# A selective-scan kernel: the loads of delta * x issued from ScalarE's queue, right behind an exponential, with six tiles in place of five

## The chip, the cores and the metric

The kernel runs as one program on one core of a Trainium2 chip. The metric is the time of one execution on the device in microseconds (us); three executions of the kernel before gave 13694.4, 13700.04 and 13704.54 us, a median of 13700.04 us. The engines are called as in the profile: PE (TensorE, matrix products), DVE (VectorE), ACT (ScalarE), POOL (GpSimd) and SP (SyncE, which here only issues DMAs). Each has an instruction stream of its own, worked off in order[...].

## The reference, cut to what matters

Four layers are computed one after the other on a batch of four 64 x 64 images with 128 channels. Layers 0 and 1 hold a selective scan in four directions; layers 2 and 3 (a gated neighbourhood message and a neighbourhood attention) are not touched by the change. The scan, for every image, direction k, channel d and state n (16 states):

```python
def step(h, t):
    x_t, d_t, B_t, C_t = t
    h = jnp.exp(d_t[..., None] * A) * h + (d_t * x_t)[..., None] * B_t[:, :, None, :]
    return (h, jnp.einsum('bkdn,bkn->bkd', h, C_t))
```

Here d_t is delta = softplus(...), x_t the convolved input, and the sequence has 64 * 64 = 4096 positions in each direction. Layer 0 has 128 channels, layer 1 has 256.

## The kernel before, in words

**Tiling.** A task is one image and one block of 128 channels of one layer: 4 images x (1 + 2) blocks make 12 tasks. A task has 16 steps (4 directions x 4 pieces of 1024 positions), a step has 16 units. A unit is 8 channels x 16 states = 128 partitions by 1024 positions. So there are 12 x 16 x 16 = 3072 units, worked in order u = 0, 1, 2, ... by `Scans.run` (line 567).

**One unit.** Five things happen to a unit, each on another engine:

- `load(u)` (line 429, the DMA on line 436) brings delta * x of the unit's 8 channels from DRAM, each row repeated for the 16 states: a tile `dub` of 128 x 1024 f32, 512 KB. The rows lie in the DRAM tensor `dud`, which was stored for the whole step (line 401).
- `times_b(u)` (line 443, POOL) multiplies `dub` by B (`repB`) into one half of a pair tile `h` (three pairs in rotation).
- `decay(u)` (lines 451 and 453) spreads delta over the partitions with two products on PE into the PSUM tile `da` (two in rotation), and ACT takes the exponential in place.
- `scan(u)` (line 462, DVE) runs the recurrence along the 1024 positions over `da` and the half of `h`; after every second unit DVE multiplies the pair by C (line 472).
- `add_up`, `keep` and `save` sum over states on PE, copy sums and end states on ACT.

**Order of emission.** Nothing reorders instructions: each engine's stream is the order in which the Python code emits. Iteration u of `run` emits `scan(u)`, `times_b(u+3)`, `save`, `decay(u+2)`, `add_up`, `keep`, then pieces of the preparation of a later step (`prepare`, 22 units ahead) and pieces of "side" work (the layers' projections, convolutions and norms), and at its very end `load(u+6)`. A small planner (`Plan`, `Lane`) decides from estimated times which pieces are emitted when, and when a store that was posted is emitted. `load(u)` of the first unit of a step first emits any preparation store still posted (`plan.flush("prep")`).

**DMAs.** Before, every DMA of the program is issued by SP, so SP's stream mixes the 3072 `dub` loads with stores and loads of the preparation (`dud`, `dp<-parts` twelve for each step, `xdd`, `repB`) and of the side work (`pad`, `szd`, `xcd`, ...). SP waits in order: a DMA that waits keeps all later ones back. There are two kinds of wait. A `dub` load waits until its tile is free: with five tiles, `load(u+6)` waits for `times_b(u+1)`. And the framework hands eight completion semaphores to the DMAs in turn, in the order of emission, whichever engine issues; a DMA waits until the one that held its semaphore before, that is the eighth DMA before it, has landed. The records of the trace show this turn: the semaphores of successive DMAs are 101 to 108, then 101 again.

The two functions and their caller, with the lines as the profile counts them:

Of the kernel before, what the change touches and what calls it, by code (L numbers as in the profile page):

```python
# [219 lines left out]
class ScanWeights:  # L220
# [27 lines left out]
    def load(self):  # L248

        nct, most = self.nct, max(TILES)  # L250
        tile = self.pool.tile([P, most * ND * (H + P)], F32, name="xpdt", tag="xpdt", bufs=1)
        self.xp = tile[:, 0 : nct * ND * H].rearrange("p (t k h) -> p t k h", t=nct, k=ND)
        at = most * ND * H
        self.dtw = tile[:, at : at + ND * nct * P].rearrange("p (k c) -> p k c", k=ND)
        self.nc.sync.dma_start(out=self.xp, in_=self.d_xp)
        for i in range(HALVES):
            self.nc.sync.dma_start(out=self.dtw[i * H : i * H + self.rank], in_=self.d_dtw)
# [19 lines left out]
class Scans:  # L277
# [151 lines left out]
    def load(self, u):  # L429
        t, step, jj, j, g = self.unit(u)  # L430
        if g == 0:
            self.plan.flush("prep")
        dud = t.prepared[step]["du"]
        dub = self.live["dub", u] = self.tile("dub", 5)
        src = bass.AP(dud.tensor, dud.offset + 8 * g * TS, [[0, NS], [TS, 8], [1, TS]])
        self.nc.sync.dma_start(out=dub, in_=src)

    def times_b(self, u):
        t, step, jj, j, g = self.unit(u)
# [127 lines left out]
    def run(self, between):  # L567

        total = NU * len(self.tasks)
        first = self.tasks[0]  # L570
        first.W.load()
        for _ in self.fetch(first):
            pass
        for _ in self.prepare(first, 0):
            pass
        self.plan.start()
        pieces, fetch, fetched = Lane(self.plan, "prep", iter(())), iter(()), 0
        for u in range(-7, total):
            if u >= 0:
                self.scan(u)  # L580
            if 0 <= u + 3 < total:
                self.times_b(u + 3)
            if u >= 0 and u % NG == 0:
                self.bring_c(u)
            if u > 0 and u % 2 == 0:
                self.save(u // 2 - 1)
            if 0 <= u + 2 < total:
                self.decay(u + 2)
            if u > 0 and u % 2 == 0:
                self.add_up(u // 2 - 1)  # L590
            if u > 0 and u % 8 == 0:
                self.keep(u - 1)
            if u > 0 and u % 8 == 1:
                self.sum_so_far(u - 1)
            even, eighth, first_one = u % 2 == 0, u % 8 == 1, u % NG == 0
            self.plan.slot(
                u, 1.6 * even + 1.0 * eighth + 2.0 * first_one, 0.25 * even + 0.7 * (u % 8 == 0)
            )
            ahead, rest = divmod(u + AHEAD, NG)
            if rest == 0:  # L600
                while pieces.step():
                    pass
                self.plan.flush("prep", "rep")
            if rest == 0 and 0 < ahead < total // NG:
                n, step = divmod(ahead, NU // NG)
                if step == 0 and self.tasks[n].W is not self.tasks[n - 1].W:
                    self.tasks[n].W.load()
                if step == 0 and fetched < n:
                    fetch, fetched = self.fetch(self.tasks[n]), n
                    for _ in range(self.tasks[n].W.nct):  # L610
                        next(fetch, None)
                pieces = Lane(self.plan, "prep", self.prepare(self.tasks[n], step))

            n, step = divmod(ahead + 1, NU // NG)
            if step == 0 and fetched < n < len(self.tasks) and self.tasks[n - 1].x_done:
                fetch, fetched = self.fetch(self.tasks[n]), n
            next(fetch, None)
            while (pieces.count < rest - 4 or pieces.fits()) and pieces.step():
                pass
            if u >= 0:  # L620
                n, i = divmod(u, NU)
                if self.later:
                    self.later.pop(0)()
                between(n, i)
            if 0 <= u + 6 < total:
                self.load(u + 6)
        self.add_up(total // 2 - 1)
        self.save(total // 2 - 1)
        self.keep(total - 1)
        while self.later:  # L630
            self.later.pop(0)()


class Side:
# [142 lines left out]
    def halves(self, load):  # L777

        tiles = []

        def start(n):
            pad = self.tile("pad", shape=(P, HW // 2 + 2, HW), bufs=2)
            load(pad, n)
            tiles.append((pad, self.nc.now + ROWS_LANDING))

        start(0)
        return tiles, start

    def depthwise(self, w, bias, src, dst):
# [12 lines left out]
        def load(pad, m):  # L802
            i, half = divmod(m, 2)
            for dy in range(3):
                self.rows(pad, slice(dy * n, (dy + 1) * n), src[i * n : (i + 1) * n], half * HW // 2 + dy - 1, HW // 2)

        tiles, start = self.halves(load)
        for m in range(8):
            i, half = divmod(m, 2)
# [817 lines left out]
def layer2(tc, C, nb, x_in, x_out, d_w, d_rel, d_v, beside):  # L1627
    with ExitStack() as es:
# [11 lines left out]

        with tc.manual_schedule():
            run(statistics(0, range(8)))
            E.roots([E.rstd])
            run(project(0, range(4)))
            beside()

# [24 lines left out]
            third, second, last = halves[-3:]  # L1671
            gates = E.gates(out, last[2], [third[2]["var"]], [])
            run(merged(gates, E.finish(*third) + E.outputs(*second)))
            run(E.gather(*last, alone=True))
            E.roots([second[2]["var"]])
# [509 lines left out]
```

## Time and profile before

| What | Value |
|---|---|
| median of three runs | 13700.04 us |
| the profiled execution's own time | 13702.12 us |
| its span, first to last instruction | 13699.8 us |
| the stretch from the first to the last scan | 204.7 to 11443.2 us (11238.5 us) |
| PE, DVE, ACT, POOL busy over the span | 73%, 86%, 58%, 72% |
| mean granted TensorE clock | 0.737 |
| DMA busy share over the span | 73.6%, 181 GB/s |

How to read it: "busy" is the time in which an engine works on an instruction; instructions that only wait, branch or issue a DMA are not counted. A group line names the source line, the engine, the operation, what it writes and reads, the count, then busy time and the mean of one in ns, then the idle time of the engine just before these instructions and what ended most of it. A line of waits reads: who waited, on which line, for whom, microseconds in total, number of times, the longest. "SPq" is SP's queue, that is, the waiting or issuing of DMAs. Layers 0 and 1 fill the time up to some 11,450 us, and layers 2 and 3 the rest.

### The profile page before, as it was taken

To read this page: it belongs to the slowest core of one execution; us is meant where nothing else is said; L and a number is where in the kernel's file an instruction comes from. 1 tells how busy PE (TensorE), PEld (TensorE's weight loads), DVE (VectorE), ACT (ScalarE), POOL (GpSimd) and SP (SyncE) were. 2 spreads that over 40 slices of the span, in tenths; PEclk is the share of its full clock that TensorE was granted. 3 is DMA by queue.
4 is the path that set the end of the run, shared out by engine and by line. 5 is a ranking of instruction groups with operands and counts; after the bars stand their busy time and mean duration, and the time that the engine had idled before them with its cause. 6 is when DMAs were issued, how large, how long until landed. Compare 5 with 4: busy or idle time off the path is not lost. (4 is left out here: it accounts for less than half of the span.)

```text
span 13699.8 us, 121257 instructions
## 1 busy us (share of the span) xinstructions
PE 10024.2 (73%) x37178; PEld 2510.6 (18%) x37178; DVE 11766.7 (86%) x6980; ACT 7913.4 (58%) x10594; POOL 9928.8 (72%) x4754
## 2 busy tenths in 40 slices
PE   5777777777777777767777677777777776666688
PEld 1111111111111111111111111111111111111455
DVE  3998899989999899989999899999999994577555
ACT  3666566655665466645665555555555554665577
POOL 3787788878887788868887888888888884355200
PEclk7666767776777776667777777777777776888899
DMA  5888888898888888888889888878888784234300
GB/s 153 204 213 217 208 207 219 214 216 201 204 219 207 193 216 202 211 212 199 196 215 220 210 197 199 203 192 202 202 197 201 193 194 107 70 97 107 73 20 17
DMA packets 877057, 2474.92 MB, mean 181 GB/s; under 512 B 142455, under 2 KB 164095, under 8 KB 868215
## 3 DMA queue, kind: packets, MB, share of 16 engines
q1 hardware_dynamic: 876407, 2467.18, 73.6%
q8 instruction: 295, 4.83, 0.2%
q14 instruction: 355, 2.91, 0.1%
HBM read 2043.34 MB, written 272.37 MB: 169 GB/s over the span
## 5 line engine op out<-in xcount | busy, mean ns | idle before, releaser
L443 POOL TENSOR_TENSOR h<-dub,repB 128x1024 f32<-128x1024 f32 x3072 | 7176.1, 2357 | 1307.6 <-DMA dub<-dud 945.6
L462 DVE TENSOR_TENSOR_SCAN h<-da,state,h 128x1024 f32<-128x1024 f32 x2304 | 5324.5, 2340 | 493.6 <-POOL h L443 225.2
L453 ACT ACTIVATE da<-da,av 128x1024 f32<-128x1024 f32 x3072 | 3339.6, 1088 | 2955.6 <-PE da L451 2937.7
L451 PE MATMUL da<-dp,spread 96*128 96x512 bf16 x6144 | 2521.9, 504 | 2285.6 <-DVE h L462 2221.2
L472 DVE TENSOR_TENSOR hc<-h,C 128x2048 f32<-128x2048 f32 x1536 | 3513.6, 2288 | 115.9 <-PE C L492 42.9
L547 PE MATMUL yps<-hc,gather 128*32 128x512 f32 x12288 | 2444.3, 880 | 5.6 <-DVE hc L472 5.6
L462 DVE TENSOR_TENSOR_SCAN h<-da,h 128x1024 f32<-128x1024 f32 x768 | 1731.6, 2280 | 353.4 <-POOL h L443 250.3
L451 PEld LDWEIGHTS <-spread 96*128 96x128 bf16 x6144 | 550.1, 107 | 5618.7 <-issue 5484.7
L97 POOL TENSOR_TENSOR delta<-delta,low 128x1024 f32<-128x1024 f32 x192 | 451.5, 2352 | 553.2 <-ACT low L97 499.0
L97 PE MATMUL ms<-d,wts 128*128 128x512 f32 (+3 forms) x900 | 674.2, 876 | 229.7 <-POOL d L97 137.2
L97 ACT ACT_TABLE_LOAD x600 | 769.8, 1283 | 16.2 <-PE ms L97 5.4
L97 PE MATMUL ms<-xd,xpdt 8*128 8x512 f32 (+1 forms) x768 | 626.9, 907 | 134.3 <-ACT xd L97 33.8
L97 ACT CAST parts<-delta 128x1024 bf16<-128x1024 f32 x384 | 400.7, 1043 | 435.3 <-POOL delta L97 409.4
L1896 POOL COPY wide_total<-total 128x128 f32<-128x128 f32 x128 | 37.6, 293 | 828.1 <-DVE total L1894 641.7
L97 ACT ACTIVATE low<-ms,av 128x512 f32<-128x512 f32 x384 | 264.0, 687 | 528.2 <-PE ms L97 507.5
L530 PE MATMUL yps<-y,ident 128*128 128x512 f32 x576 | 508.2, 972 | 78.9 <-ACT y L557 78.7
L97 POOL TENSOR_TENSOR low<-delta,xc 128x1024 f32<-128x1024 f32 x192 | 502.6, 2617 | 2.7
L1452 ACT ACTIVATE hid<-hid,relb 128x1024 f32<-128x1024 f32 x288 | 323.0, 1146 | 264.6 <-DVE hid L1447 264.4
L1865 ACT ACTIVATE s<-s,least 128x512 f32<-128x512 f32 x512 | 372.4, 727 | 178.6 <-DVE least L1852 177.4
L1852 DVE CUSTOM_DVE_ANT_0 s<-sps,bias 128x512 f32<-128x512 f32 x512 | 323.5, 687 | 175.6 <-PE sps L1841 164.6
L1554 POOL TENSOR_TENSOR acc<-acc,part 128x1024 f32<-128x1024 f32 x120 | 313.3, 2617 | 214.1 <-DVE part L1548 186.9
L547 PEld LDWEIGHTS yps<-hc,gather 128*32 128x32 f32 x12288 | 282.4, 127 | 1007.8 <-issue 999.6
(284 smaller groups left out, 11119.9 us busy)
## 6 DMA issues: line engine op xcount, KB each, us to landing
dub<-dud SPq DMA_DIRECT2D x3072, 512.0 KB
dp<-parts SPq DMA_DIRECT2D x2304, 64.0 KB
repB<-xdd SPq DMA_DIRECT2D x192, 512.0 KB
dud<-low SPq DMA_DIRECT2D x192, 512.0 KB
spread<-gd SPq DMA_DIRECT2D x72, 1024.0 KB
pad<-xid SPq DMA_DIRECT2D x192, 256.0 KB
szd<-o SPq DMA_DIRECT2D x96, 256.0 KB
xcd<-o SPq DMA_DIRECT2D x96, 256.0 KB
```

Source lines behind the costliest of these rows:

```text
L97: return call(*args, **kw)
L443: self.nc.gpsimd.tensor_mul(dbu, self.live.pop(("dub", u)), t.prepared[step]["B"])
L451: self.nc.tensor.matmul(da[:, cols], self.C.spread[:, jj, :], dp[:, j, cols], start=True, stop=True)
L453: self.nc.scalar.activation(da, da, AF.Exp, scale=t.W.a[:, at : at + 1])
L462: nc.vector.tensor_tensor_scan(h[:, way], da[:, way], h[:, way], 0.0 if step % NSTEP == 0 else t.states[step - 1][:, u % NG : u % NG + 1], ...
L472: nc.vector.tensor_mul(hc, pair, t.prepared[step]["C"].unsqueeze(1).to_broadcast([P, 2, TS]))
L530: self.nc.tensor.matmul(self.like_part(yps, k), self.C.ident, self.part(t.y, k, c, b), start=True, stop=False)
L547: self.nc.tensor.matmul(out, self.C.gather[jj], rhs, start=False, stop=jj == 3)
L1452: nc.scalar.activation(hid, hid, AF.Gelu, bias=self.relb[:, m, t : t + 1])
L1554: (nc.vector if alone and pair else nc.gpsimd).tensor_add(acc, acc, part)
L1852: self.nc.vector.tensor_tensor_reduce(out=self.live["s", n][:, h, :], in0=self.live["sps", n][:, h, :], in1=self.bias[case][:, h, :], scal ...
L1865: self.nc.scalar.activation(s, s, AF.Exp, scale=-1.0, bias=self.live["least", n][:, h : h + 1], accum_out=self.live["total", n][:, h : h + 1],
```

## The change

The loads of `dub` are issued by ACT in place of SP; they are emitted right behind `decay(u+2)`, so that in ACT's stream `load(u+6)` stands behind the exponential of unit u+2; and `dub` has six tiles in place of five. [...]

```diff
         if g == 0:
             self.plan.flush("prep")
         dud = t.prepared[step]["du"]
-        dub = self.live["dub", u] = self.tile("dub", 5)
+        dub = self.live["dub", u] = self.tile("dub", 6)
         src = bass.AP(dud.tensor, dud.offset + 8 * g * TS, [[0, NS], [TS, 8], [1, TS]])
-        self.nc.sync.dma_start(out=dub, in_=src)
+        self.nc.scalar.dma_start(out=dub, in_=src)
...
             if 0 <= u + 2 < total:
                 self.decay(u + 2)
+            if 0 <= u + 6 < total:
+                self.load(u + 6)
             if u > 0 and u % 2 == 0:
                 self.add_up(u // 2 - 1)
...
                 between(n, i)
-            if 0 <= u + 6 < total:
-                self.load(u + 6)
         self.add_up(total // 2 - 1)
...
-    nc = bacc.Bacc("TRN2", target_bir_lowering=False, num_devices=1)
+    nc = bacc.Bacc("TRN2", target_bir_lowering=False, num_devices=1, dynamic_dma_scratch_size=1024)
```

No computing instruction is added or removed, and the number and size of the DMAs stay (7804 in all). With the loads, the turn of the eight semaphores moves: the order of emission of SP's remaining DMAs and the loads is still one common order.

## The prediction

> **What bounds the kernel now.** I read the groups of the page first, then the waits within the stretch of the scans (204.7 to 11443.2 us), then SP's own waits there, then a timeline.
>
> ```profile
> L443 POOL TENSOR_TENSOR h<-dub,repB 128x1024 f32<-128x1024 f32 x3072 | 7176.1, 2357 | 1307.6 <-DMA dub<-dud 945.6
> L462 DVE TENSOR_TENSOR_SCAN h<-da,state,h 128x1024 f32<-128x1024 f32 x2304 | 5324.5, 2340 | 493.6 <-POOL h L443 225.2
> L453 ACT ACTIVATE da<-da,av 128x1024 f32<-128x1024 f32 x3072 | 3339.6, 1088 | 2955.6 <-PE da L451 2937.7
> L472 DVE TENSOR_TENSOR hc<-h,C 128x2048 f32<-128x2048 f32 x1536 | 3513.6, 2288 | 115.9 <-PE C L492 42.9
> ```
>
> DVE sets the pace: the scans (5324.5 + 1731.6 us) and the products by C (3513.6) fill nearly all of 11238.5 us. In that stretch the trace gives DVE 10461 us busy, so the 185.5 us before its first scan set aside, only 777 us can be won from its idle time. Whom it waits for:
>
> ```profile
> DVE h L462 <- POOL h L443: 475.6, 146, 185.5
> ...
> DVE h L462 <- ACT da L453: 300.9, 310, 13.4
> ```
>
> POOL's 475.6 us contain that first wait of 185.5 (start-up): 290.1 us in 145 waits remain. I followed each of the 146 back to the times_b it waited for: in 92 of them, 418.3 us, that times_b had itself just waited for a `dub` load. Less the first: **232.8 us of DVE's idle time come from late loads**. Why are they late?
>
> ```profile
> SPq L436 <- POOL h L443: 3498.2, 1609, 13.7
> SPq L436 <- DMA dub<-dud: 476.1, 332, 7.4
> SPq L412 <- POOL parts L97: 342.1, 160, 8.7
> SPq L729 <- ACT o L97: 335.8, 87, 10.5
> SPq L401 <- POOL low L97: 294.5, 130, 5.4
> SPq L356 <- ACT xd L97: 275.7, 60, 10.9
> ```
>
> SP stands 3498 us before loads whose tile is not free; meanwhile stores that are ready queue behind. It stands some 1250 us (the last four lines) for data of other stores; meanwhile loads queue behind. Then they go out in bunches. In the trace a load lands 7.47 us after its issue in the median (4.75 at 10%, 12.38 at 90%); with nothing else in flight it takes 4.65, with one other load 4.79, with three 8.21, with four 9.92, about 1.7 us for each further one.
>
> ```profile
> 5824.60 14.11 SPq L412 DMA_DIRECT2D dp<-parts  x9
> ...
> 5846.24 2.34 POOL L443 TENSOR_TENSOR h<-dub,repB 128x1024 f32<-128x1024 f32 x1 [6.15 <-DMA dub<-dud]
> ...
> 5848.61 2.35 DVE L462 TENSOR_TENSOR_SCAN h<-da,state,h 128x1024 f32<-128x1024 f32 x1 [4.67 <-POOL h L443]
> ```
>
> For 14 us SP issues nothing but stores of `dp`; the next load goes out at 5839.44; POOL then waits 6.15 us and DVE 4.67.
>
> [...] The trace agrees on bandwidth being no reason for a gain (DMA is 0.81 to 0.88 busy in the scans), but here it is waiting, not issue time, that SP loses. [...] of ACT's 4479 semaphore instructions 3355 start while ACT is still at work, one 5 ns after an exponential of 1088 ns began.
>
> **The change part by part.**
>
> *Waiting for the tile.* With six tiles `load(u+6)` needs times_b(u). The exponential of u+2, in front of it, waits for PE's `da`, which waits for scan(u), which needed times_b(u). In the trace times_b(u) had ended before that exponential started for every unit, by at least 3.0 us. So this wait costs nothing on ACT, and SP loses its 3498 us. With five tiles it would have been times_b(u+1): that is what the sixth tile buys.
>
> *Issue.* 3072 issues leave SP and come to ACT's sequencer: 0.543 us each on SP (median 0.520), 1669 us. Placed behind an exponential of 1.088 us, they pass beneath it if the sequencer runs on, as shown above. Bounds: 0, and, if each were serial, 0.54 us for each of the 310 scans that wait for ACT already, 168 us. A gain is excluded: nothing is taken off ACT. I take 10 us.
>
> *When the load starts.* It no longer follows POOL but DVE. The start of exp(u+2) lies 2.46 us (median) after the issue of load(u+6) in the trace, but it is earlier in a quarter of the units, by 7.2 us at 5%: the ones SP kept. From there to scan(u+6) is 17.0 us in the median, 14.7 at 1%. A load that takes 5.5 us (between 4.79, one other load in flight, and 6.39, one load and two other DMAs) and times_b (2.36) need 7.9; even 10 us for the load fit. Set against the times_b starts of the trace, landings of 5.5 us would be late for 113 units, 127 us; of 7.5 us for 405, 573 us; the trace has 945.6 in 373. Late POOL time became late DVE time at 232.8/945.6 = 0.25, so 31 to 141 us remain of the 232.8. I take 45, hence **-188 us**; bounds -92 and -290 (all of POOL's waits). POOL's lead over DVE gets shorter by about 2.5 us; with 2.3 us for each of its other operations I add 15 us.
>
> *SP's other DMAs.* They no longer wait behind loads. PE waited 34.4 us for `dp<-parts` (9 times, the longest 15.8), ahead of the exponential and the scan. I take -30; bounds 0 and -60.
>
> *The new wait.* `load(u+6)` also waits for the eighth DMA before it in the common order, and for the first unit of a step for `dud`. What is queued behind it: the next exponential, the copies of states and sums, the preparation. DVE waits for the exponential, POOL for the state copies and `low`. I laid the new order over the landings of the trace: at the start of exp(u+2) that eighth DMA had not landed in 777 of 3066 cases, 2933 us in all, 390 of them `dp<-parts` (1348 us). Before it shifts a scan, a delay must use up ACT's idle time to the next exponential and that one's lead (together 3.4 us in the median). What exceeds it: 757 us in 293 cases. This is too high, because those landings were late through the queue which now goes. If SP's remaining DMAs go out as soon as their data are there and land in the lower quartile of their times (5.28 for a load), 243 cases, 405 us, remain, 22 beyond the cover; with medians (7.47) 606, 1525 us, 212 beyond. I take 45; bounds 20 and 757.
>
> Sum: 10 - 188 + 15 - 30 + 45 = -148; POOL's 57 us of other waits come partly from a lead lost to loads earlier, and SP's issue of the stores of preparation in time helps `low` and `delta`: I take another -30. **About -180 us.** The profiled execution ran 13702.1 us (span 13699.8 and 2.3 around it), 2 above the median of 13700.0, so the sum goes onto the median: **13520 us**, with 13430 to 13600 for this case alone. What is late next is the exponential (300.9 us), and it stays.
>
> **The rivals.**
>
> *A, the release of SP is worth more.* All of POOL's 290 us and 60 for `dp` go, and the waits on ACT cost 20: 13370. For it: the 1250 us that loads stood behind stores, and the 14.7 us from the exponential to the scan. Against: POOL's own side work makes part of the 57 us.
>
> *B, the transfers are bound by the DMA engines.* They are over 80% busy in the scans[...]. Loads then still take 7.5 us, 141 us of lateness remain, and 212 us are lost on ACT: 10 - 92 + 15 - 30 + 212 = +115 at worst; where half of the ACT waits survive, 13700, no change. Against: the bunches, not the mean of some 208 GB/s, make 7.5 us; a load alone takes 4.65.
>
> *C, slower: ACT is held at the eighth DMA.* A load on ACT waits for an SP store that waits for POOL or ACT, and the exponential stands behind. It decides once more than about 190 us (the other terms) of the 757 come through, a quarter. At half, 380 us: 13890. For it: twelve `dp` in a row for each step and only eight semaphores. Against: with SP free these stores go out when their data are ready.
>
> That the change does not do what it says is excluded: in the changed order of instructions all 3072 loads stand on ACT behind their exponential.
>
> **How the numbers follow.** Chances: forecast 0.57, A 0.16, B 0.12, C 0.15. A measurement can tell about 0.2% (27 us) from no change. Faster: 0.57 + 0.16 + 0.03 of B = 0.76; same: 0.08 of B and 0.01 of C; slower: the rest of both, 0.15. The range runs from A to just past B, 13370 to 13720, and leaves out most of C and the end of A.
>
> **What would show it.** DVE's wait for POOL should fall from 475.6 to 230 to 290 (185 of it start-up), the issue-to-landing median of loads to 5 to 6 us, SP's wait on L436 vanish; ACT's exponentials keep their 1088 ns with DVE's wait for them at 300 to 350. I am wrong if loads still take over 7 us, or if ACT stands long at L436 and DVE's wait for L453 doubles.

## The result, and the profile after

The changed kernel takes **13719.61 us** in the median of 20 runs, the kernel before 13696.91 us in 20 runs measured beside it: a ratio of 1.0016, 95% interval [1.0009, 1.0023]. That is 23 us more, just clear of no change, and not the 180 us less that were forecast. (One of the 20 executions, at a clock of 0.515 and 18499 us, is left out of the ratio.) The profiled execution took 13725.39 us with a span of 13723.1, 23.3 longer than before.

The groups of the changed kernel's page that answer to those shown of before (busy, mean ns of one | idle just before them, and what ended most of it):

```profile
L443 POOL TENSOR_TENSOR h<-dub,repB 128x1024 f32<-128x1024 f32 x3072 | 7184.5, 2359 | 1123.7 <-DMA dub<-dud 738.3
L462 DVE TENSOR_TENSOR_SCAN h<-da,state,h 128x1024 f32<-128x1024 f32 x2304 | 5327.6, 2340 | 483.5 <-ACT da L453 374.1
L453 ACT ACTIVATE da<-da,av 128x1024 f32<-128x1024 f32 x3072 | 3339.6, 1088 | 2664.7 <-PE da L451 2455.9
...
L472 DVE TENSOR_TENSOR hc<-h,C 128x2048 f32<-128x2048 f32 x1536 | 3513.6, 2287 | 123.3 <-PE C L492 51.6
```

The work is the same: each of these means agrees with before within 2 ns. What changed is the end of the scans' line: most of their idle time is now ended by ACT's exponential, where POOL's product was named before. The waits of DVE in the stretch of the scans say how much (us, times, longest):

```profile
DVE h L462 <- ACT da L453: 514.4, 441, 12.0
DVE h L462 <- ACT state L483: 103.1, 82, 8.2
DVE hc L472 <- PE C L492: 51.6, 43, 4.7
DVE h L462 <- POOL h L443: 45.3, 50, 2.7
```

Here the wait before the very first scan (177.7 us) is already set aside; it falls to ACT now and fell to POOL before. Two lines of before that have not been shown yet:

```profile
DVE h L462 <- ACT state L483: 57.3, 66, 6.3
DVE hc L472 <- PE C L492: 42.9, 36, 4.2
```

Against before: POOL 290.1 to 45.3, a gain of 244.8; the exponential 300.9 to 514.4, `state` 57.3 to 103.1, `C` 42.9 to 51.6, together a loss of 268.0. The difference, 23.2, and 12 us more of busy time on DVE, less some 5 of gaps too small to be put down to anyone, are the 30.2 us by which the stretch grew (11238.5 to 11268.7); what lies outside it became 6.9 shorter. So POOL's waits fell by more than was forecast, and something of the same size has eaten the gain. (A wait is put down to whoever came last, so where ACT is late it can cover a late POOL: a part of the 244.8 may only be hidden.)

Who holds ACT? Its own waits, changed kernel, some lines:

```profile
ACT state L483 <- DMA dp<-parts: 127.5, 37, 8.2
...
ACT da L453 <- DMA dp<-parts: 72.3, 22, 7.9
ACT L97 <- DMA dp<-parts: 41.4, 15, 6.1
```

None of these three reads `dp`: an exponential, a copy of a state and a load of a function table cannot need it. The instruction ahead of them in ACT's stream does wait: a load of `dub`, whose completion semaphore is still held by another DMA, often a `dp` store of SP. All waits of ACT in the stretch that a landing ended sum to 540 us in 182 cases (before: 48.6 in 20). In these lines `dp` has 319 of the 540. The name in such a line is inferred, and it can be the DMA that took the semaphore over afterwards. Followed by the semaphore that each load itself waited for, `dp` has about 273, still half of the whole. One such case of the changed kernel, in order of time (start, duration; some lines left out):

```profile
4704.63 12.79 SPq L412 DMA_DIRECT2D dp<-parts  x11
...
4707.82 1.09 ACT L453 ACTIVATE da<-da,av 128x1024 f32<-128x1024 f32 x1 [3.78 <-PE yps L547]
...
4708.17 0.60 PE L451 MATMUL da<-dp,spread 96*128 96x512 bf16 x2
...
4713.96 0.52 ACTq L436 DMA_DIRECT2D dub<-dud  x1
4714.53 0.59 ACT L557 COPY y<-yps 128x512 f32<-128x512 f32 x1 [5.62 <-DMA dp<-parts]
...
4715.01 1.10 ACT L453 ACTIVATE da<-da,av 128x1024 f32<-128x1024 f32 x1
...
4716.21 2.35 DVE L462 TENSOR_TENSOR_SCAN h<-da,state,h 128x1024 f32<-128x1024 f32 x1 [3.78 <-ACT da L453]
```

The load that belongs behind the exponential of 4707.82 uses the semaphore of the first of these eleven `dp` stores. By the trace's records that store lands at 4713.94, 9.3 us after its issue, and the load goes out at 4713.96. The next exponential had its input from PE by about 4708.8; it stands behind the load and a copy and starts at 4715.01, 6.2 us after its input was there and 1.05 us after the load went out, and DVE waits 3.78 us for it: the small load has become a gate.

How often is the gate shut? In the changed kernel 424 loads go out more than 0.3 us after the start of the exponential ahead of them, 1053 us in sum; these are called late loads below. For 405 of them, 1003 us, the trace shows the load going out as the DMA that held its semaphore lands: a `dp` store for 242 (628 us), some other DMA for 163 (375 us).

And why do these DMAs land so late? One part is their issue. SP's waits in the changed kernel:

```profile
SPq L401 <- POOL low L97: 1195.8, 158, 16.2
SPq L401 <- ACT low L97: 975.2, 118, 23.5
...
SPq L412 <- POOL parts L97: 763.7, 172, 19.2
SPq L412 <- ACT parts L97: 648.2, 110, 13.4
```

SP no longer stands at L436. It runs ahead and stands at the stores instead, for data that POOL and ACT have not made yet: for `parts` of POOL 763.7 us (before 342.1), for `parts` of ACT 648.2 (before 55.4).

The other part is the flight, the time from issue to landing. For 366 of the 405 loads the DMA that held the semaphore had already gone out when the exponential began. The 405 DMAs take 5.72 us to land in the median, and a quarter of them over 8.59; those that are not `dp` stores take 8.69 in the median.

One may suspect a ring: ACT is held by a store, and the store waits for a tile that ACT has yet to write. The traces leave it little room. Landings put off ACT's own writing of `parts` and `low` by some 35 us each. And POOL's waits for ACT's copies, here of the changed kernel and then of `sp_six_early` (below), where no load stands in ACT's queue, are nearly the same:

```profile
POOL delta L97 <- ACT low L97: 579.4, 132, 11.4
POOL h L443 <- ACT state L483: 309.2, 145, 12.6
```

```profile
POOL delta L97 <- ACT low L97: 572.4, 127, 11.8
POOL h L443 <- ACT state L483: 302.0, 143, 11.6
```

(before: 463.0 and 196.2).

### The profile page after: what moved, and what is told of

Its sections match the earlier page's. It is cut to its first block, busy times and chain, and to the rows that moved or that the text cites. A ratio compares the mean times of both kernels' runs of the same rounds, so it can differ in the third digit from the quotient of the medians.

```text
span 13723.1 us, 120864 instructions
## 1 busy us (share of the span) xinstructions
PE 10006.6 (73%) x37178; PEld 2509.1 (18%) x37178; DVE 11779.5 (86%) x6980; ACT 7908.4 (58%) x10594; POOL 9938.8 (72%) x4754
## 5 line engine op out<-in xcount | busy, mean ns | idle before, releaser
L453 ACT ACTIVATE da<-da,av 128x1024 f32<-128x1024 f32 x3072 | 3339.6, 1088 | 2664.7 <-PE da L451 2455.9
L451 PE MATMUL da<-dp,spread 96*128 96x512 bf16 x6144 | 2506.5, 501 | 2103.8 <-DVE h L462 2054.8
L472 DVE TENSOR_TENSOR hc<-h,C 128x2048 f32<-128x2048 f32 x1536 | 3513.6, 2287 | 123.3 <-PE C L492 51.6
L451 PEld LDWEIGHTS <-spread 96*128 96x128 bf16 x6144 | 548.1, 108 | 5420.5 <-issue 5279.0
```

Of the source, the lines that this page charges most:

```text
L451: self.nc.tensor.matmul(da[:, cols], self.C.spread[:, jj, :], dp[:, j, cols], start=True, stop=True)
L453: self.nc.scalar.activation(da, da, AF.Exp, scale=t.W.a[:, at : at + 1])
L472: nc.vector.tensor_mul(hc, pair, t.prepared[step]["C"].unsqueeze(1).to_broadcast([P, 2, TS]))
```

## The experiments

Every ratio below is to the kernel before, run beside it (its medians lay between 13686 and 13697 us). Where two kernels were not run beside each other, the distance between them is the difference of their distances from the kernel before; by the intervals it is good to some 15 us. The columns "exp", "state" and "POOL" are DVE's waits within the stretch of the scans, in us, without the one before the first scan; the last column is the idle time of ACT in that stretch that a landing ended.

| kernel | median us | ratio [95%] | exp | state | POOL | ACT by landings |
|---|---|---|---|---|---|---|
| before | 13697 | 1 | 301 | 57 | 290 | 49 |
| changed | 13720 | 1.0016 [1.0009, 1.0023] | 514 | 103 | 45 | 540 |
| act_five | 13709 | 1.0016 [1.0009, 1.0022] | 498 | 93 | 53 | 519 |
| sp_six_end | 13687 | 0.9998 [0.9990, 1.0006] | 297 | 53 | 291 | 47 |
| sp_six_early | 13631 | 0.9956 [0.9944, 0.9969] | 330 | 78 | 168 | 45 |
| act_six_end | 13850 | 1.0111 [1.0095, 1.0126] | 553 | 110 | 120 | 670 |
| act_nodp | 13483 | 0.9843 [0.9830, 0.9857] | 293 | 79 | 55 | 202 |
| sp_nodp | 13429 | 0.9804 [0.9791, 0.9817] | 268 | 71 | 38 | 21 |
| act_lag3 | 13717 | 1.0015 [1.0007, 1.0023] | 534 | 63 | 45 | 558 |
| sp_lag3 | 13677 | 0.9987 [0.9981, 0.9994] | 300 | 36 | 284 | 108 |
| act_dram | 14127 | 1.0318 [1.0304, 1.0332] | 880 | 111 | 61 | 541 |
| act_pair | 14619 | 1.0681 [1.0666, 1.0695] | 999 | 426 | 101 | 1442 |
| sp_pair | 14178 | 1.0361 [1.0347, 1.0375] | 632 | 74 | 374 | 111 |
| act_pair4 | 13821 | 1.0100 [1.0086, 1.0114] | 541 | 147 | 85 | 411 |
| sp_pair4 | 13739 | 1.0038 [1.0024, 1.0052] | 387 | 71 | 211 | 67 |
| mix4 | 13657 | 0.9974 [0.9965, 0.9984] | 404 | 92 | 102 | 316 |
| mix8 | 13678 | 0.9986 [0.9977, 0.9994] | 408 | 104 | 119 | 222 |
| sp_dp_spread | 13640 | 0.9969 [0.9956, 0.9981] | 417 | 82 | 68 | 28 |
| sp_eight_early | 13625 | 0.9955 [0.9943, 0.9968] | 345 | 75 | 152 | 28 |
| sp_eight_spread | 13603 | 0.9938 [0.9926, 0.9951] | 382 | 85 | 69 | 20 |

My theory after the result (H in the expectations): ACT is held in front of its loads by the shared turn of eight semaphores, because SP's stores wait for data. Rivals, with letters that change from run to run: the second queue slows the transfers, or the sixth tile, the place, or the issue itself is what costs.

### One part at a time: queue, place, tile

`sp_six_early` is the changed kernel with its loads back on SP:

```diff
-        self.nc.scalar.dma_start(out=dub, in_=src)
+        self.nc.sync.dma_start(out=dub, in_=src)
```

> The changed kernel with the loads on SP again: six tiles, emitted at the new place. ACT then holds nothing. If six tiles and the place alone free SP (the tile is always free when the exponential two units ahead has its turn, but SP does not wait for that exponential), loads can be early, SP waits for tiles some 1500 us or more, POOL's waits make DVE idle 200 to 290 us, time 13680 to 13720. Theory H predicts DVE's wait for da at the 301 us of before, not 514.

Measured: 13631 us, 0.44% below the kernel before and faster than expected. Its waits of DVE (the first line still contains the 184.3 us before the first scan):

```profile
DVE h L462 <- POOL h L443: 352.2, 93, 184.3
DVE h L462 <- ACT da L453: 329.7, 309, 13.6
DVE h L462 <- ACT state L483: 77.8, 66, 16.3
```

So the new place and the tile bring 61 us, and moving the loads to ACT costs 84 us on top. DVE's waits tell the same: from `sp_six_early` to the changed kernel those for the exponential rise by 184.7 and those for `state` by 25.3, and those for POOL fall by 122.6; together 87.4.

From the kernel before to `sp_six_early`, POOL's waits fall by 122.3, but the exponential's rise by 28.8 and those for `state` by 20.5. I read this as lateness of ACT that POOL's lateness had covered; it would have come in the changed kernel too.

`sp_six_end` is the kernel before with the sixth tile (and the smaller `dynamic_dma_scratch_size`, the last line of the diff, which makes room for it) alone, `act_six_end` the changed kernel with its load moved back to the end of the iteration, `act_five` the changed kernel with five tiles:

```diff
-        dub = self.live["dub", u] = self.tile("dub", 6)
+        dub = self.live["dub", u] = self.tile("dub", 5)
```

> Only the sixth tile: loads on SP at the old place. Of the 61 us that SP with six tiles at the new place gains, the tile should bring the larger part, since it is the tile's release that starts a load: 13640 to 13670. If the place (before the stores of the same iteration) is what counts, 13680 to 13700.

> The changed kernel with the load emitted at the old place, the end of the iteration, still on ACT with six tiles: it now stands behind ACT's pieces of side work and some stores posted in that iteration stand before it. Theory H: the load waits more often for the eighth DMA before it and the hold no longer passes beneath an exponential: 13740 to 13800. Theory R: place is of no account, 13700 to 13740.

> The changed kernel with five tiles. A load on ACT then waits for times_b of the unit u+1, which POOL has nearly always done (in the changed kernel times_b runs 4.1 us ahead of the scan in the median), so ACT is held a little more: 13720 to 13770. If the wait for the tile never counts, 13720; if POOL is often just behind, over 13800.

Measured: the sixth tile alone does nothing (0.9998), where I had expected it to bring the larger part, and with five tiles the changed kernel is what it was (1.0016 both, 455 late loads in place of 424): the tile is not what the loads on ACT wait for. At the end of the iteration the loads on ACT cost 163 us against the same on SP (13850 to 13687). There 1872 loads go out more than 0.3 us after the start of their exponential, 5310 us in sum; much of this is ACT's other work, which now stands between the two, for ACT's idle time by landings rises only to 670. Two of ACT's lines there:

```profile
ACT state L483 <- DMA dp<-parts: 235.1, 79, 6.6
ACT da L453 <- DMA dp<-parts: 200.9, 66, 8.0
```

### The stores of dp taken out

`act_nodp` and `sp_nodp` leave out the twelve `dp` stores of every step but the first one, so that all later steps take the first step's delta; the second has its loads on SP.

```diff
...
-        for i in range(12):
+        out["delta"] = getattr(self, "dp0", None)
+        for i in range(0 if out["delta"] is not None else 12):
```

> The changed kernel with the stores of dp left out after the first step (all later steps read the first step's delta, so part of the computation is left out and 12 of some 40 DMAs of a step are gone; all other work stays). Theory H (the loss is ACT held at loads whose eighth DMA before has not landed, mainly dp stores): ACT's idle time ended by landings falls from 540 to about 220 us, DVE's wait for da without the start from 514 to about 400, for the state copy from 103 to about 60; time about 13570 to 13600. Theory R (the end of POOL's lateness merely lays bare that ACT is late by its own side work): DVE's wait for ACT stays at 500 to 600 and the time within 40 us of 13720.

> The control: the same leaving out of the dp stores, with the loads on SP, six tiles, at the new place (13631 us with the dp stores). Theory H: SP's loads no longer queue behind bunches of dp, so this gains too, by 30 to 80 us, to 13550 to 13600, while DVE's wait for da stays near 330. If the dp stores only matter through the bytes and places they take on the DMA engines, both kernels gain the same.

Measured: 13483 and 13429. ACT's idle time by landings falls from 540 to 202, the late loads from 424 to 76 (211 us), and DVE's wait for the exponential goes to 293.2, what it was before the change:

```profile
DVE h L463 <- ACT da L454: 293.2, 317, 12.8
DVE h L463 <- ACT state L484: 78.8, 64, 8.1
DVE h L463 <- POOL h L444: 54.7, 45, 4.8
```

All 3072 loads are still issued by ACT here, so the issue itself costs the exponential little (268 in `sp_nodp`). Both kernels win far more than expected, and of the 230 us on ACT, 201 are won on SP as well: near to what the second expectation said for the case that `dp` matters by the bytes and places it takes. The distance between the queues only falls from 84 to 55 us. The stores of `dp` hold ACT; they are not all that holds it, and they cost in either queue.

### Fewer or later stores

`act_lag3` and `sp_lag3` (the latter made from the kernel before) emit every posted store 10.8 us later; its data should then be there when SP comes to it:

```diff
-            if chain in chains or due <= self.now and chain not in held:
+            if chain in chains or due + LAG <= self.now and chain not in held:
...
```

> The changed kernel, but every posted store of the preparation and of the side work is emitted 10.8 us (three units) later. Theory H (ACT is held: a load behind an exponential waits until the eighth DMA before it has landed, and that one is a store on SP that was emitted before its data were ready): stores no longer wait long on SP, ACT's idle time ended by landings falls from 540 us to under 200, DVE's wait for ACT's da from 692 to about 500 (178 of it the start), time 13720 - 200 = about 13520. Theory I (the cost is the issue itself, 0.52 us for each of 3072 loads on ACT): nothing of that changes, 13700 to 13740. Theory W (POOL's and ACT's side work merely run later, whatever is done): 13700 or slower.

> The control: the kernel before, loads on SP with five tiles, with the same 10.8 us of delay for posted stores. If SP's waits for other stores' data were what made loads late in the kernel before, DVE's wait for POOL falls from 476 us towards 250 and the time by 100 to 200 us, to 13500 to 13600, without ACT. If the 3498 us before loads whose tile is not free are what counts, it stays within 40 us of 13700.

Measured: no change on ACT (1.0015), 0.13% less on SP. The lag did not do what it was made for: SP still stands 564.1 us for `parts` of POOL and 432.3 for those of ACT, and 445 loads are late, 1065 us. So the run is no test of the theory. On SP, the waits for `parts` of POOL fall from 342.1 to 200.0, but SP then stands longer before loads whose tile is not free (4487.1 us, before 3498.2), and DVE's waits for POOL stay at 284. Why the lag had so little effect on ACT is open; the program also has a point where a step emits all that is still posted, whatever its time.

`act_dram` brings `dp` by way of DRAM, three stores and one load in place of twelve stores.

> The changed kernel, but delta's three parts go to dp by way of DRAM: three stores and one load for each step in place of twelve small DMAs (same result, 768 KB more for each step, 6% more bytes). Theory H with dp as its main carrier (319 of the 540 us that ACT idles until landings): ACT's idle time until landings falls by 200 to 320 us, DVE's wait for da by about 100 to 150, time 13570 to 13620. Theory I: no change from 13720, or a few us slower by the bytes.

Measured: 14127. The idea fails for a reason of its own: `dp` comes too late. PE waits 406.1 us for it (53 times, up to 32.7), as the store lands 9.0 us and the load 6.7 us after issue, one behind the other. It tells nothing of the holds.

### Half as many loads

`act_pair` and `sp_pair` bring two units in one load of 1 MB; for that, `dud` is stored with its channel pairs side by side, by two stores of 64 partitions with an outermost dimension of two.

```diff
+            dst = bass.AP(dud.tensor, dud.offset + 64 * i * TS, [[TS, 2], [2 * TS, 32], [1, TS]])
+            nc.sync.dma_start(out=dst, in_=low[64 * i : 64 * i + 64, :])
...
```

> The changed kernel with one load of 1 MB for two units (dud laid out so that the two units' rows of a channel lie side by side, stored in two halves; four pair tiles, that is eight units): 1536 loads in place of 3072, and the turn of eight semaphores reaches back 4.2 units in place of 3.4. Theory H: fewer loads meet a DMA that has not landed, 250 to 300 in place of 424; ACT's idle time until landings falls from 540 to about 350, time about 13600 to 13650. The issue cost (theory I) is halved too, but the trace showed it beneath the exponential. Theory R: 13700 to 13740.

> The same pairs with the loads on SP at the new place. If loads late through SP's own order are what makes POOL late (168 us of DVE's time with six tiles at the new place), eight units of room and half the loads bring that to under 80 and the time from 13631 to about 13560; DVE's wait for da stays at 300 to 340.

Measured: 14619 and 14178, both far slower. The `dud` store took 17.1 and 14.2 us to land (5.7 in the changed kernel, 4.2 in `sp_six_early`), so these kernels are no test of pairs. They are, by accident, one of a slow store in the turn: ACT's idle time by landings goes to 1442 us. Some of ACT's lines in `act_pair`:

```profile
ACT da L462 <- DMA dp<-parts: 294.7, 49, 14.8
ACT y L566 <- DMA dp<-parts: 216.9, 50, 10.7
ACT da L462 <- DMA dud<-low: 165.6, 21, 19.2
```

To see whether the form of the store is what makes it slow, `act_pair4` and `sp_pair4` store the same bytes by four stores of 32 partitions, with an outermost dimension of 32 in place of two.

```diff
+            dst = bass.AP(dud.tensor, dud.offset + (64 * (i // 2) + i % 2) * TS, [[2 * TS, 32], [1, TS]])
+            nc.sync.dma_start(out=dst, in_=low[32 * i : 32 * i + 32, :])
...
```

> The loads of two units are one DMA of 1 MB, issued by ACT behind the even unit's exponential (four pair tiles), and dud is stored by four stores of 32 partitions each, interleaved by channel pairs[...] (the earlier pair kernel's store with two halves took 17.1 us). Theory H (what the change loses is ACT held in its queue before a load): only half as many loads can hold ACT, so the distance to the same kernel with its loads on SP falls from 88 us (13720 against 13631) to some 30 to 60 us; about 13700 us, between 13620 and 13850, ACT idle by landings 250 to 350 us in place of 540. Rival R (the loss comes from the second queue's transfers being served against SP's): the distance stays at 80 to 100 us. If the four stores take as long as the two halves did, both kernels stand above 13900 and the pair tells nothing.

> The same, with the loads on SP at the new place. Theory H: near the kernel with single loads on SP at the new place (13631 us), 13600 to 13760. Rival R: 80 to 100 us below the same kernel with its loads on ACT.

Measured: the stores land in 4.9 and 4.7 us, where the halves took 17.1 and 14.2. The halves carry 256 KB each, the four stores 128 KB each; a plain store of 512 KB takes 5.7 us in the changed kernel, so the bytes alone do not make it slow. What in the form of the halves does was not shown. Against these kernels, the slow store costs 794 us with the loads on ACT and 435 with the loads on SP: the same store hurts more where a computing engine stands behind it. The times are 13821 and 13739, and the distance between the queues is 82 us: what the rival expected, not the theory. But ACT's idle time by landings did not halve as the theory had to assume; it is 411 of 540 us. Half the loads are held for almost as long; my reading of these two sums, which no run isolates, is that a hold lasts until the store lands, whatever number of loads stands behind it. So the number of loads is not the measure, and the run doesn't decide between the two.

### Only the endangered loads taken off ACT

`mix4` gives those four loads to SP that are emitted after a `dp` store, and leaves the others on ACT; `mix8` eight.

```diff
+            self.wary = 4
             nc.sync.dma_start(
...
-        self.nc.scalar.dma_start(out=dub, in_=src)
+        wary = self.wary = getattr(self, "wary", 1) - 1
+        (self.nc.sync if wary >= 0 else self.nc.scalar).dma_start(out=dub, in_=src)
```

> As the changed kernel, six tiles and the new place, but the four loads that are emitted after a dp store are issued by SP and only the others by ACT: 1206 loads on SP, 1866 on ACT. In the finished order the eighth DMA before a load on ACT is a dp store for 205 loads in place of 814; for the loads on SP it is for 700. Theory H (the change loses by ACT standing behind stores whose data are late): ACT's idle time ended by landings falls from 540 us to 150 to 300, DVE's waits for ACT from 514 to 360 to 430, POOL's part stays below 130, and the time lies between 13560 and 13640 us. Rival R (the loss comes from having a second queue with more than a thousand loads in it at all): 13670 to 13730.

> The same with the eight loads after a dp store on SP: 1974 on SP, 1098 on ACT, of which 119 stand behind a dp store. Theory H: ACT's idle time by landings falls further, 100 to 200 us, but more loads stand behind SP's stores again: POOL's part 80 to 160, 13560 to 13640 us. Rival R: between the mixture of four and the loads all on SP, 13640 to 13700.

Measured: `mix4` 13657 us. All work and all transfers are kept, 1866 loads still go through ACT's queue, and 58 of the 84 us are back. That is more than the share of the loads that moved (1206 of 3072, 39%). ACT's waits for `dp` are a fifth to a half of what they were:

```profile
ACT da L455 <- DMA dp<-parts: 24.9, 6, 8.2
ACT state L485 <- DMA dp<-parts: 24.6, 10, 5.0
...
ACT L97 <- DMA dp<-parts: 18.8, 6, 4.9
```

DVE's wait for the exponential (404) and POOL's part (102) lie where the theory put them; the landings (316) and the time are just above its bounds, and the time is below the rival's. `mix8` misses the theory's time: the landings fall on to 222, but the exponential stays at 408 and POOL's part rises to 119, and at 13678 it is slower than `mix4` and than all loads on SP. Why the exponential doesn't follow there stays open.

### A version that beats both

Since the loads on SP at the new place are the better kernel, three more ask what still makes them late. `sp_dp_spread` is `sp_six_early` with the `dp` stores one in each half unit; `sp_eight_early` has eight tiles in place of six; `sp_eight_spread` has eight tiles and the `dp` stores 0.3 unit apart, from a unit earlier on. The lines of the last:

```diff
...
+        base = max(begin + 8 * UNIT, self.plan.done)
...
-            post("rep", lambda part=part, j=j: own(part, j), begin + (9 + 0.7 * i) * UNIT)
+            post("dp", lambda part=part, j=j: own(part, j), base + 0.3 * i * UNIT)
...
```

> Loads on SP, six tiles, new place, and the twelve dp stores of a step emitted one for each half unit from the time their data are planned to be ready, in place of bunches (60 times twelve in a row between two loads become 19, 719 times two). If bunches of dp are what makes loads late on SP, POOL's part of DVE's idle time falls from 168 to about 70 us and the time from 13631 to about 13540. If it is the dp stores' bytes and number, it stays at 13600 to 13640.

> Loads on SP at the new place, eight tiles in place of six. Theory H: with six tiles at the new place a load already leaves 6.1 us ahead of the exponential in the median, and POOL's late half (130.5 us of DVE's waits) comes from loads that stand behind other stores' data, not from tiles: within 0.1% of six tiles, 13620 to 13645 us. Rival T (tiles still hold SP, and stores behind them): DVE's waits for POOL fall by 60 us or more, 13560 to 13590.

> The same with eight tiles, and the twelve dp stores of a step spread from eight units after its beginning (or the end of its preparation), 0.3 unit apart, so that they leave earlier than in the run with six tiles, where DVE's waits for ACT rose by 87 us. Theory H (bunches of dp in front of loads make the late loads): POOL's waits fall to 70 to 100 us as with six tiles, and the waits for ACT stay below 350: 13540 to 13600 us. If dp still comes late: 13620 to 13650.

Measured: 13640, 13625 and 13603. Eight tiles alone change nothing against six (0.9955 and 0.9956). Spreading takes POOL's waits from 168 to 68 as expected, but `dp` then comes late to PE: its waits for `dp` before `da` rise from 19.0 to 171.8 us, and the exponential's from 330 to 417. Begun earlier, with eight tiles, they are 120.9 and 382:

```profile
DVE h L466 <- ACT da L457: 382.3, 321, 11.0
DVE h L466 <- POOL h L445: 251.5, 45, 182.4
DVE h L466 <- ACT state L487: 84.9, 70, 13.0
```

(182.4 of POOL's are the first wait.) With a ratio of 0.9938 [0.9926, 0.9951], `sp_eight_spread` is the fastest complete kernel of this study, and its loads are on SP.

## Why the prediction failed

**Late loads: right, and low.** The step took 188 us off DVE's waits for POOL, with 290 as the bound; 244.8 came off. Loads land after 5.57 us in the median in place of 7.47 (forecast 5 to 6). Whether the loads' own queue or their new times of issue shortened the flight was not shown. The two queues in the changed kernel's page:

```profile
q10 hardware_dynamic: 442368, 1610.81, 48.9%
q1 hardware_dynamic: 434039, 856.37, 23.8%
```

They make 72.7%, where the one line of before, `q1`, had 73.6%, and the mean is 180 GB/s after 181: no bandwidth was gained. Rival B's mark, loads that still take 7.5 us, did not appear, and SP's stores are hardly slower: `dp` stores land after 4.60 us in the median and 7.17 at 90% (before 4.39 and 7.72), though `dud` stores take 5.74 (before 4.87).

**The wait for the tile: right, and more than right.** It costs ACT nothing that can be measured, but with five tiles neither (1.0016 in both). The step's last sentence, that the sixth tile buys this, is wrong (`act_five`).

**Issue: right.** The two lines of L436 in the changed kernel (duration min/median/max in ns; the second is the wait for the semaphore ahead of it):

```profile
L436 ACTq DMA_DIRECT2D dub<-dud x3072: 521/522/1537, 186.6 to 11446.9; - x192
L436 ACTq EVENT_SEMAPHORE  x2645: 17/17/9046, 186.1 to 11446.9; - x189
```

522 ns pass beneath the exponential: from its start to the next work of ACT there are 1013 ns at the lower quartile, in both kernels. Loads even go out while the exponential ahead of them still waits: one in a hundred more than 2.75 us before it starts. The harm lies in the loads that wait themselves: in the case shown above the copy and the exponential behind such a load start 0.57 and 1.05 us after it went out, and the longest single wait for a semaphore on this line was 9.0 us.

**SP's other DMAs: wrong by 30.** The 34.4 us that the prediction read for PE were those of the whole execution: 16.7 of them, with the longest of 15.8, lie before the first scan, and only 17.7 were there to be won. With the weight loads of L451, PE's waits for `dp` were 36.4 us in the stretch and are 37.5. SP comes to these stores sooner, their data do not. The further 30 us for `low` and `delta` did not come either: POOL's wait for `low` rose from 463.0 to 579.4.

**The new wait: the step that failed.** It was put at 45 us, with 757 as the upper end. The terms that took its place sum to 268. Three things are in it.

- *The time of landing.* I took SP's stores to go out "as soon as their data are there" and to land in the lower quartile: 405 us late in 243 cases. The trace has 1053 us in 424 cases. Take the changed kernel's own issues, late data included, and let each of these DMAs land in no more than the lower quartile of its kind: 376 us in 190 cases would remain, close to the forecast; with no more than the median, 584 in 276. So the size was lost in the spread of the landings. They are hardly slower than before (above), but late loads are made by the long flights, and one low value for all leaves these out. On the same scale, medians had given 1525 us and 212 beyond the cover; 1053 lies 0.58 of the way from 405 to 1525, so about 130 us of the 268, an estimate.
- *The echo.* A hold also delays ACT's other work, and what PE, POOL and DVE make of it. My sum pushed each delay through once. Followed back in the trace, 114 us of DVE's waits for the exponential belong to unbroken runs of ACT that began at a landing (before: 4). The rest of the rise, about 100 us, shows as later products of PE, POOL and DVE; a part of it is the next point, and that what is left is the echo of the holds is my reading, which no run isolates.
- *What was covered.* Some 58 us (exponential, `state`, `C`) appear in `sp_six_early` too, where ACT isn't held: taking POOL's lateness away lays ACT's bare. The prediction said that the exponential "is late next", and then booked the whole gain. These three overlap and do not add up to 268.

So rival C had the mechanism, and a third of its 757 us came through, past its threshold of 190; as POOL's waits fell by more than was forecast, the loss is 23 us and not C's 190. Its argument "for", `dp` stores in a row and eight semaphores, was right. The argument against it, "with SP free these stores go out when their data are ready", was the mistake: a store that has gone out has still to land, and ACT stands behind it until then (366 of the 405 DMAs had gone out before the exponential began). The sign named in advance came: DVE's wait for the exponential should have stayed at 300 to 350 us and went to 514. That 13719.6 us lies inside the stated range, by 0.4 us, is luck: its upper end was drawn for B. A sentence of mine on the kernel before has to be mended too: the turn of the semaphores follows the order of the finished program and not quite that of emission. With the loads on ACT the emission has 60 places with twelve `dp` between two loads, the finished program at most nine; the eighth DMA before a load is a `dp` store for 814 loads.

What is shown: ACT is held by landings (the trace), moving only the endangered loads off it wins 58 of 84 us (`mix4`), and the sixth tile is not the cause; nor do stores land much later than before. What stays open: how much a second queue costs by itself, for `act_pair4` gave the distance that this rival expected, and without `dp` 55 us between the queues remain; how the 26 us that `mix4` doesn't win back divide; and why `mix8` gains less.

## What to carry to other kernels

A DMA that is put on a busy engine's queue can bring its waits with it, the wait for its completion semaphore among them: here 405 of 3072 loads, 1003 us in sum, went out as the DMA that held their semaphore landed. Before moving it, look up which DMA held that semaphore last, on whose data that one waits, how long the longest flights of its kind are, and what stands behind the moved DMA. Free the waiting engine and look what it runs into next: here SP, released from its loads, arrived early at stores without data (763.7 us for `parts` of POOL, before 342.1). And undo queue and place separately: the place, with six tiles, was worth 61 us, the queue cost 84.

## What the runs showed of the hardware that was not expected

- DMA issues of 522 ns on ACT passed beneath an activation of 1088 ns (1013 ns from its start to ACT's next work at the lower quartile, as in the kernel before), and one load in a hundred went out more than 2.75 us before the activation ahead of it.
- The store of a 256 KB half with an outermost dimension of two took 17.1 us to land, as four plain stores of 128 KB 4.9 us each: a layout that looks like a detail was worth 794 us of the whole with the loads on ACT, and 435 with the loads on SP.
- The landings of one kind of DMA spread widely: in the changed kernel `dp` stores of 64 KB take 2.03 us at 10%, 4.60 in the median and 7.17 at 90%, and the DMAs that held a load took 5.72 us in the median, a quarter of them over 8.59.
